# Four graph layers on one core: layer 2's product with the squared adjacency as three reduced-precision passes over split operands

## The chip, the cores and the metric

The kernel runs on one core of a Trainium2 chip. TensorE (PE) does the matrix products and writes to PSUM, which has eight banks of 512 fp32 columns per partition; VectorE (DVE), ScalarE (ACT) and GpSimd (POOL) do the rest; SyncE (SP) issues nearly all transfers. The metric is the device time of one launch in microseconds (us), lower is better. Each engine works through its own list of instructions in order and waits on semaphores for the others.

## The reference

The input x has 32 matrices of 512 nodes by 128 features; adj is one 512 x 512 matrix, about an eighth of it nonzero. Four layers follow one another, each of the form x = x + gnn(relu(layernorm(x))). All of it is fp32. Layer 0 is an attention over adj, layer 1 a Chebyshev filter over adj, layer 3 an attention with a tanh-limited score, masked by adj. The change touches layer 2. There `coeff` and `A` are both adj, so the weights are adj squared element by element:

```python
def _L2_gnn_ref(H, A, coeff, psi_w, psi_b, phi1_w, phi1_b, phi2_w, phi2_b):
    weights = coeff * A
    features = jax.nn.relu(jnp.einsum('bnd,de->bne', H, psi_w) + psi_b)
    messages = jnp.einsum('nm,bnd->bmd', weights, features)
    phi_in = jnp.concatenate((messages, H), axis=-1)
    h = jax.nn.relu(jnp.einsum('bnk,kd->bnd', phi_in, phi1_w) + phi1_b)
    return jnp.einsum('bnd,de->bne', h, phi2_w) + phi2_b
```

and the call is `x = x + _L2_gnn_ref(h, adj, adj, ...)`.

## The kernel before

**Tiles.** The 32 matrices are handled in 16 pairs q; x stays in SBUF for the whole run. A matrix is four tiles of 128 nodes by 128 features. Layers 0 and 1 combine two pairs (a block r of four matrices, eight blocks), layers 2 and 3 go pair by pair.

**Products with a 512 x 512 matrix.** Such a product is written as a 2 x 2 block product with seven multiplications instead of eight (the Winograd form of Strassen's scheme). `sum_steps` (L301) makes sums of the left matrix's quarters once, into a tile with the tag "sums"; `right_steps` (L345) makes four differences of the right operand for each pair, in tiles with the tag "rt", on POOL. `products` (L365) then runs seven steps in the order of `ORDER`, which share three PSUM banks a, c and d: a later step adds to a bank that an earlier one has filled, after an eviction has read it. `mixed` (L393) is the form for one pair: each step is two FP32 matmuls of 256 columns (L379), and the evictions (ACT copies L400 and L408, DVE additions L402 to L419) put the result together.

**Layer 2 for a pair** (`layer2`, a generator that stops at each `yield`): normalise (ACT, L247); turn the result to feature-major with DVE transposes and two trips through DRAM on SP's queue (L283 to L292); multiply with psi, add the bias on DVE and apply relu on ACT (L1063, L1064); four POOL differences (L356); the seven-step product with sq (L379), which yields msgT; phi_2's bias onto x on POOL (L1075); phi_1 (L1080, L1081), whose relu writes over msgT (L1082); phi_2 (L435) and the addition to x (L1086); statistics for the next layer (L227).

**The square.** `square` (L1139) is a generator too. Its first step loads adj into the tile sq (tag "square", four buffers of 8 KB per partition), in an order of rows that suits the transposition by 32 x 32 blocks, and loads the transposed adj, needed by layer 3 as a mask, into adjTx. Four further steps multiply one quarter of sq with itself on POOL and copy it back; then come the four sums. All this happens while layer 1 still runs.

**Order.** Layer 0 keeps its source order. From there on a list-scheduling framework sets the order of each engine's instructions from the order in which the program emits them and from what it holds to be ready; buffers of a tag are handed out as they come free. The program emits in rounds: each round advances every active generator by one step, the older ones first, and starts one more. `square` starts in the sixth round, one round after layer 1's block 3:

```python
    waiting = [[next_layer, layer1(1), layer0_stats()]]
    for r in range(2, NQ // 2):
        waiting += [[], [layer1(r)]]
    waiting[5].append(square())
```

In a steady round of layer 2, PE has pair q's product, then psi for pair q+1, phi_2 for pair q-1 and phi_1 for pair q.

**Buffers that the change touches.** "rt": six tiles of 2 KB per partition, used for the differences in layers 0, 1 and 2 and for a temporary of layer 1. "quad": two tiles of about 8 KB, used by layer 0's g, layer 1's w (the weighed features of a block, copied from PSUM by ACT at L958), layer 2's msgT and layer 3's operands. "square": four tiles of 8 KB, used among others by adj_s, x1T (layer 1's product), sq, adjTx and layer 3's exponentials. "hs": six tiles of 2 KB.

Of the kernel before, what the change touches and what calls it, by code (L numbers as in the profile page):

```python
# [8 lines left out]

F32 = mybir.dt.float32  # L10
F16 = mybir.dt.float16
BF16 = mybir.dt.bfloat16
AF = mybir.ActivationFunctionType
OP = mybir.AluOpType
AX = mybir.AxisListType

P = 128
QR = 32
NQR = P // QR
NEG = 9000000000000000.0  # L20
EPS = 1e-5


@with_exitstack
def kernel(
# [37 lines left out]
    nc = tc.nc  # L63
    B, N, D = x.shape
    NT = N // P
# [4 lines left out]
    const = ctx.enter_context(tc.tile_pool(name="const", bufs=1))  # L70
# [3 lines left out]
    work = ctx.enter_context(tc.tile_pool(name="work", bufs=4))  # L74
    bounce = ctx.enter_context(tc.tile_pool(name="bounce", bufs=4, space=bass.MemoryType.DRAM))

    def bank(name):
        return psum.tile([P, 512], F32, tag="bank", name=name)

# [7 lines left out]
    def square_tile(name):  # L87
        return const.tile([P, NT, N], F32, tag="square", name=name, bufs=4)

    def crossed(ap):  # L90

        return ap.rearrange("p (a b c) -> p b a c", a=NT, b=NQR)

    def split(ap):
        return ap.rearrange("p (a b c) -> p a b c", a=NT, b=NQR)

    def load_crossed(dst, src):
        for b in range(NQR):
            tc.keep_in_program_order(
                nc.sync.dma_start(dst[:, b, :], src.rearrange("(a b c) w -> b a c w", a=NT, c=QR)[b]))  # L100
# [91 lines left out]
    shift, scale = {}, {}  # L192
# [105 lines left out]
    H = N // 2  # L298
    sums = {}

    def sum_steps(mat, name, eng=nc.gpsimd):  # L301

        a11, a12 = mat[:, 0:2, 0:H], mat[:, 2:4, 0:H]
        a21, a22 = mat[:, 0:2, H:N], mat[:, 2:4, H:N]
        extra = const.tile([P, 3, 2, H], F32, tag="sums", name=f"sums_{name}", bufs=2)
        s1, s2, s4 = extra[:, 0], extra[:, 1], extra[:, 2]
        sums[name] = {1: a11, 2: a12, 3: s4, 4: a22, 5: s1, 6: s2, 7: a21}
        for out, op, p, q in ((s1, OP.add, a21, a22), (s2, OP.subtract, s1, a11),
                              (a21, OP.subtract, a11, a21), (s4, OP.subtract, a12, s2)):
            tc.keep_in_program_order(eng.tensor_tensor(out, p, q, op))  # L310
            yield
# [6 lines left out]
    def att_sums():  # L318

        a11, a12 = attT[:, 0:2, 0:H], attT[:, 2:4, 0:H]  # L320
        a21, a22 = attT[:, 0:2, H:N], attT[:, 2:4, H:N]
        extra = const.tile([P, 3, 2, H], F32, tag="sums", name="sums_att", bufs=2)
        s1, s2, s4 = extra[:, 0], extra[:, 1], extra[:, 2]
        sums["att"] = {1: a11, 2: a12, 3: s4, 4: a22, 5: s1, 6: s2, 7: a21}
        yield
        for out, p, bank_of, half, first in ((s1, a21, 2, 1, False), (s2, s1, 0, 0, False),
                                             (a21, a21, 0, 0, True), (s4, s2, 2, 0, True)):
            for k in range(2):
                b = pt[bank_of + k][:, half * H : half * H + H]
                if out is s1:  # L330
                    nc.vector.tensor_add(out[:, k], b, p[:, k])
                elif first:
                    nc.vector.tensor_sub(out[:, k], b, p[:, k])
                else:
                    nc.vector.tensor_sub(out[:, k], p[:, k], b)
            yield

    def right_blocks(half, name, engs):

        right = {}  # L340
        for _ in right_steps(half, name, engs, right):
            pass
        return right
# [21 lines left out]
    def products(name, form, left, right, evict, order=ORDER, on=lambda k, p: p):  # L365


        banks = {}
        for k, g, first in order:
            if first:  # L370
                banks[g] = bank(f"p_{name}_{g}")
            form(on(k, banks[g]), left[k], right[k], first)
            evict(k, banks[g])
            yield
# [18 lines left out]
    def mixed(name, left, right, dst):  # L393

        m1 = dst[:, 0, H:], dst[:, 1, :H], dst[:, 1, H:]

        def evict(k, p):
            p = p[:, :H]
            if k == 1:
                nc.scalar.copy(m1[0], p)  # L400
            elif k == 6:
                nc.vector.tensor_add(m1[1], p, m1[0])  # L402
            elif k == 7:
                nc.vector.tensor_add(m1[2], p, m1[0])
            elif k == 5:
                return
            elif k == 2:
                nc.scalar.copy(dst[:, 0, :H], p)  # L408
            elif k == 4:
                nc.vector.tensor_add(dst[:, 0, H:], p, m1[0])  # L410
            elif k == 3:
                nc.vector.tensor_add(dst[:, 1, :H], p, m1[1])

        def evict2(k, p):
            evict(k, p)
            if k == 5:
                held.append(p)
            if k == 7:
                nc.vector.tensor_add(dst[:, 1, H:], held[0][:, :H], m1[2])  # L419

        held = []
        return products(name, by_feature, left, right, evict2)

    def at(hT, b):
        return lambda t: hT[:, t, b, :]
# [13 lines left out]
    def quad_tile(name):  # L439
        return work.tile([P, 2, 2 * N + 2 * NT], F32, tag="quad", name=name, bufs=2)  # L440
# [36 lines left out]
    adjT_d = bounce.tile([N, N], F32, tag="adjT", name="adjT_d", bufs=1)  # L477
# [38 lines left out]
    for t in range(NT):  # L516
        for s in range(t + 1):
            nc.tensor.matmul(pi[:, t : t + 1], upto[:, s, blk(t)], rch[:, s : s + 1],
                             start=(s == 0), stop=(s == t))

    p = bank("p_qk_t")
# [28 lines left out]
    for i in range(3):  # L550
        eh = prep.tile([P, NK], BF16, name=f"eh_{i}")
        nc.gpsimd.tensor_copy(eh, ecoln)
        part = prep.tile([P, NK], F32, name=f"part_{i}")
# [11 lines left out]
    for t in range(NT):  # L565
        s = prep.tile([P, NE], F16, tag="lt", name=f"lt_{t}", bufs=2)
# [3 lines left out]
        for j in range(NT):  # L570
            nc.tensor.matmul(pg[j // 2][:, j % 2, :], m[:, t, blk(j)], of_row[:, t, :],
                             start=(t == 0 and j % 2 == 0), stop=(t == NT - 1), skip_group_check=True)
    pb = bank("p_known")[:, : 2 * NK].rearrange("p (k e) -> p k e", e=2)
    for kk in range(NK):
        for t in range(NT):
            nc.tensor.matmul(pb[:, kk, :], of_row[:, t, blk(kk)], known[:, t, :],
                             start=(t == 0), stop=(t == NT - 1))
# [17 lines left out]
    for kk in range(NK):  # L595
        for j in range(NT):
            nc.tensor.matmul(pw[kk][:, j * P :], pgs[:, j, blk(kk)], upto[:, j, j * P :],
                             start=(j == 0), stop=(j == NT - 1), skip_group_check=True)
# [10 lines left out]
    for kk in range(NK):  # L609
        s = prep.tile([P, N], F16, tag="scr", name=f"scr_c{kk}", bufs=2)  # L610
# [427 lines left out]
    def layer1_stats():  # L1038

        ln_stats(NQ - 2)  # L1040
        yield
        ln_stats(NQ - 1)
# [10 lines left out]
    def layer2(q):  # L1053
        h = normed(q)
        yield
        hT = transposed(h, f"hT2_{q}")
        yield
        yield
        feat = []
        for b in range(2):  # L1060
            pf = projected(f"p_feat_{q}_{b}", (at(hT, b), psi))
            feat.append(late.tile([P, NT, D], F32, tag="hs", name=f"feat_{q}_{b}", bufs=6))
            nc.vector.tensor_add(feat[b], pf, spread(psib, NT))  # L1063
            nc.scalar.activation(feat[b], feat[b], AF.Relu)  # L1064
        right = right_blocks(lambda J, b: feat[b][:, 2 * J : 2 * J + 2, :], f"feat_{q}", [nc.gpsimd] * 4)
        yield
        if q % 2 == 0:
            msgs.append(quad_tile(f"msgT_{q}"))
        msgT = msgs[-1][:, q % 2, : 2 * N].rearrange("p (b w) -> p b w", b=2)
        for _ in mixed(f"msgT_{q}", sums["sq"], right, msgT):  # L1070
            pass
        for b in range(2):
            for i in range(0, NT, 2):
                xi = xt[q][:, b, i : i + 2, :]
                tc.keep_in_program_order(nc.gpsimd.tensor_add(xi, xi, spread(phi2b, 2)))  # L1075
        yield
        h1T = msgT
        for b in range(2):
            ph = bank(f"p_phi1_{q}_{b}")
            nc.tensor.matmul(ph, phi1[:, 1, :], hT[:, :, b, :], start=True, stop=False)  # L1080
            nc.tensor.matmul(ph, phi1[:, 0, :], msgT[:, b], start=False, stop=True)  # L1081
            nc.scalar.activation(crossed(h1T[:, b]), split(ph), AF.Relu, bias=phi1b)  # L1082
        yield
        for b in range(2):
            po = projected(f"p_l2_{q}_{b}", (columns(h1T[:, b]), phi2))
            nc.vector.tensor_add(xt[q][:, b], po, xt[q][:, b])  # L1086
        ln_stats(q)
# [46 lines left out]
            if not final:  # L1134
                nc.sync.dma_start(out_r, xt[q][:, b])

    adjTx = []

    def square():  # L1139

        sq = square_tile("sq")
        load_crossed(sq, adj)
        adjTx.append(square_tile("adjTx"))
        load_crossed(adjTx[0], adjT_d)
        yield
        for i in range(NT):
            s = late.tile([P, N], F32, tag="hs", name=f"sq_{i}", bufs=6)
            nc.gpsimd.tensor_mul(split(s), crossed(sq[:, i, :]), crossed(sq[:, i, :]))
            nc.gpsimd.tensor_copy(sq[:, i, :], s)
        yield from sum_steps(sq, "sq")  # L1150

    next_layer = layer1(0)
    for r in range(NQ // 2):
# [8 lines left out]
    waiting[-1].append(layer2(0))  # L1162
    waiting += [[layer2(q)] for q in range(1, NQ)]
    waiting[-NQ + 7].append(layer1_stats())
    waiting += [[layer3(q)] for q in range(NQ)]
    active = []
    while waiting or active:
# [37 lines left out]
```

## Time and profile before

| what | value |
|---|---|
| time, median of 3 runs | 963.69 us (963.59 to 963.74) |
| span of the profiled execution | 961.7 us |
| granted TensorE clock, mean | 1.000 |
| HBM read / written | 44.17 / 40.89 MB |

The span is from the first to the last instruction; the runs' time is 2.0 us longer. Busy time by stage (a stage's borders are blurred, since the layers overlap):

| stage | us | PE busy | DVE | ACT | POOL |
|---|---|---|---|---|---|
| layer 0, 0 to 180 | 180 | 175.9 | 144.8 | 97.5 | 143.6 |
| layer 1, 180 to 445 | 265 | 264.1 | 150.4 | 96.4 | 107.2 |
| layer 2, 445 to 670 | 225 | 224.8 | 144.0 | 124.5 | 92.7 |
| layer 3, 670 to 962 | 292 | 288.6 | 145.2 | 150.7 | 80.3 |

All waits of PE on another engine that the profile shows sum to 4.9 us, the longest 2.0 us at the start. An FP32 matmul appears as two weight loads (PEld) and two matmul records, and the recorded durations overlap, because matmuls are pipelined: the distance between starts is the time that one takes.

### The profile page before, as it was taken

How to read it: one execution, taken by the hardware profiler on the slowest of the kernel's cores; microseconds unless marked ns; L12 is line 12 of the kernel's file. 1: busy time of each engine (PE TensorE's matmuls, PEld its weight loads, DVE VectorE, ACT ScalarE, POOL GpSimd, SP SyncE). 2: the span in 40 equal slices, each digit the busy share in tenths (PEclk: the TensorE clock that was granted, in tenths of full speed). 3: DMA queues.
4: the chain of work that ended last, by engine and by line, in shares of the span. 5: the costliest groups of instructions: out<-in, count | busy, mean ns of one | idle time of the engine just before them, and what ended most of it. 6: DMA issues, size and time to landing. Idle time of an engine off the chain costs nothing.

```text
span 961.7 us, 15152 instructions
## 1 busy us (share of the span) xinstructions
PE 953.3 (99%) x5465; PEld 780.8 (81%) x5465; DVE 584.4 (61%) x1326; ACT 469.1 (49%) x1054; POOL 423.8 (44%) x470
## 2 busy tenths in 40 slices
PE   8999999999999999999999999999999999999998
PEld 4899999898989999899877777777677777767776
DVE  8888885846536545656667665665654444444444
ACT  5865542442232233277627655444765445544553
POOL 5878987833517522513333444433032233223322
PEclk9999999999999999999999999999999999999999
DMA  9356532441341230343333433223121121211111
GB/s 252 62 166 185 160 108 84 104 110 55 102 136 45 66 88 23 110 110 96 89 99 97 126 91 85 74 82 88 56 88 56 55 77 44 72 61 45 55 33 44
DMA packets 83913, 86.04 MB, mean 89 GB/s; under 512 B 6784, under 2 KB 74624, under 8 KB 83840
## 3 DMA queue, kind: packets, MB, share of 16 engines
q1 hardware_dynamic: 83552, 84.57, 31.6%
q8 instruction: 43, 0.70, 0.3%
q10 hardware_dynamic: 288, 0.52, 0.2%
q14 instruction: 30, 0.25, 0.1%
HBM read 44.17 MB, written 40.89 MB: 88 GB/s over the span
## 4 chain that ended last, share of the span: by engine, by line
PE 96%; ACT 2%; DVE 1%; DMA 0%; POOL 0%; issue 0%; DVEq 0%; ACTq 0%
PE p_av L1125 12%; PE p_score L1110 11%; PE p_l_c L386 8%; PE p_w L435 6%; PE p_l_d L386 6%; PE p_msgT_c L379 5%; PE p_l_a L386 4%; PE p_x1T_c L379 4%; PE p_l L435 3%; PE p_feat L435 3%; PE p_hv L435 3%; PE p_qkh L1097 3%; PE p_x1T_a L379 3%; PE p_msgT_d L379 3%; PE p_g L435 3%; PE p_x1T_d L379 3%
## 5 line engine op out<-in xcount | busy, mean ns | idle before, releaser
L247 ACT ACTIVATE h<-x,sh,rs 128x128 f32<-128x128 f32 x512 | 209.2, 484 | 51.7 <-PE p_x1T_d L379 21.7
L1115 POOL TENSOR_TENSOR ex<-ex,adjTx 128x512 f32<-128x512 f32 x62 | 80.3, 1295 | 208.3 <-ACT ex L1113 202.8
L1111 ACT ACTIVATE ex<-p_score 128x512 f32<-128x512 f32 x128 | 71.9, 587 | 122.8 <-issue 113.0
L1125 PEld LDWEIGHTS p_av<-qkh_hv,ex 128*128 128x128 f32 x1024 | 118.4, 191 | 8.4 <-issue 7.4
L1125 PE MATMUL p_av<-qkh_hv,ex 128*128 128x129 f32 x1024 | 119.9, 274 | 0.0
L1110 PE MATMUL p_score<-qkh_hv,hT 128*128 128x512 f32 x256 | 115.2, 593 | 0.0
L283 DVE STREAM_TRANSPOSE hb_hT<-h 128x512 f32<-128x512 f32 x120 | 82.0, 698 | 23.7 <-ACT h L247 22.6
L1115 DVE TENSOR_TENSOR ex<-ex,adjTx 128x512 f32<-128x512 f32 x66 | 46.1, 703 | 82.0 <-ACT ex L1113 81.9
L227 DVE BATCH_NORM_STATS2 bn<-x 128x6 f32<-128x256 f32 x248 | 89.8, 419 | 0.6
L1110 PEld LDWEIGHTS p_score<-qkh_hv,hT 128*128 128x128 f32 x256 | 46.2, 190 | 46.5 <-issue 44.5
L1113 ACT ACTIVATE ex<-ex 128x512 f32<-128x512 f32 x128 | 76.7, 630 | 1.9
L356 POOL TENSOR_TENSOR rt_feat<-feat,feat 128x256 f32<-128x256 f32 x16 | 11.6, 725 | 136.4 <-ACT feat L1064 136.4
L958 ACT COPY w<-p_w 128x512 f32<-128x512 f32 x32 | 18.2, 574 | 106.1 <-PE p_w L435 106.1
L356 POOL TENSOR_TENSOR rt_w<-w,rt_w 128x512 f32<-128x512 f32 x16 | 20.4, 1273 | 110.3 <-DVE rt_w L356 92.0
L435 PE MATMUL p_w<-th,x1T 128*128 128x128 f32 x256 | 49.5, 275 | 0.0
L435 PE MATMUL p_w<-th,hs 128*128 128x128 f32 x256 | 49.5, 275 | 0.0
L435 PEld LDWEIGHTS p_hv<-vw,hT 128*128 128x128 f32 x256 | 33.6, 192 | 15.3 <-issue 8.1
L1075 POOL TENSOR_TENSOR x<-x,phi2b 128x256 f32<-128x256 f32 x64 | 44.5, 727 | 0.0
L435 PEld LDWEIGHTS p_w<-th,hs 128*128 128x128 f32 x256 | 39.9, 192 | 0.7
L1064 ACT ACTIVATE feat<-feat 128x512 f32<-128x512 f32 x32 | 20.1, 629 | 41.4 <-DVE feat L1063 41.4
L1130 DVE SCALAR_TENSOR_TENSOR x<-p_av,rsum,x 128x128 f32<-128x128 f32 x128 | 39.1, 347 | 1.9
L712 POOL TENSOR_TENSOR hd<-hT,adiag 128x512 f32<-128x512 f32 x32 | 39.6, 1274 | 0.2 <-ACT adiag L838 0.2
(238 smaller groups left out, 2039.7 us busy)
## 6 DMA issues: line engine op xcount, KB each, us to landing
d_hT<-hb_hT SPq DMA_DIRECT2D x240, 128.0 KB
hT<-d_hT SPq DMA_DIRECT2D x60, 512.0 KB
x<-in_x_dram SPq DMA_DIRECT2D x32, 256.0 KB
out_dram<-x SPq DMA_DIRECT2D x31, 256.0 KB
adjT_d<-adj_squares SPq DMA_DIRECT2D x4, 256.0 KB
sq<-in_adj_dram SPq DMA_DIRECT2D x4, 256.0 KB
adjTx<-adjT_d SPq DMA_DIRECT2D x4, 256.0 KB
adj_s<-in_adj_dram ACTq DMA_DIRECT2D x2, 256.0 KB
```

The costliest lines, as they stand in the source:

```text
L227: nc.vector.bn_stats(st[:, k].rearrange("p e s -> p (e s)"), xt[q][:, b, t : t + 2, :].rearrange("p t f -> p f t"))
L247: nc.scalar.activation(h[:, b, t, :], xt[q][:, b, t, :], AF.Relu, bias=shift[q][:, i : i + 1], scale=scale[q][:, i : i + 1])
L283: nc.vector.transpose(hb[:, :, b].rearrange("p j t r -> p t j r"), h[:, b].rearrange("p t (j c) -> p t j c", c=QR))
L379: nc.tensor.matmul(p[:, :H], b[:, k, :], a[:, k, :], start=(first and k == 0), stop=(k == 1), skip_group_check=True)
L386: nc.tensor.matmul(p[:, i * 2 * D : (i + 1) * 2 * D], a[:, k, blk(i)], b[:, k], start=(first and i == 0 and k == 0), stop=(k == 1), skip_g ...
L435: nc.tensor.matmul(p[:, blk(t)], hT(t), w, start=(i == 0), stop=(i == len(terms) - 1))
L1075: tc.keep_in_program_order(nc.gpsimd.tensor_add(xi, xi, spread(phi2b, 2)))
L1110: nc.tensor.matmul(ps, hT[:, t, b, :], qkh, start=True, stop=True)
L1111: nc.scalar.activation(ex[:, t, :], ps, AF.Tanh, scale=1.0 / (8.0 * math.sqrt(D)))
L1113: nc.scalar.activation(ex[:, t, :], ex[:, t, :], AF.Exp, scale=8.0)
L1115: eng.tensor_mul(split(ex[:, t, :]), split(ex[:, t, :]), crossed(adjTx[0][:, t, :]))
L1125: nc.tensor.matmul(po[:, i, : D + 1], ex[:, t, blk(i0 + i)], hv[:, t, :], start=(t == 0), stop=(t == NT - 1))
```

## The change

The numbers for layer 2's product are split. A value x is written as high + low, where both fit the reduced fp32 format (`float32r`) of TensorE, and the product of two such sums is put together from three products of parts: high with high, low with low, and mid with mid, where mid is a combination of the two parts (scale factors make the cross terms come out). Each part product is a matmul with `float32r` operands, 512 columns wide, and all twelve of one matrix add into one PSUM bank. The scheme of seven block products isn't used here any more.

```diff
+F32R = mybir.dt.float32r
+PARTS = ("high", "low", "mid")
+LOW = 4096.0
+DOWN = 1.0 - 1.0 / 8192.0
+UP = 1.0 + 1.0 / 4096.0
...
-        extra = const.tile([P, 3, 2, H], F32, tag="sums", name=f"sums_{name}", bufs=2)
+        extra = const.tile([P, 4, 2, H], F32, tag="sums", name=f"sums_{name}", bufs=2)
...
+    def moving_parts(x, high, low, mid):
+
+        nc.scalar.activation(high, x, AF.Copy, scale=DOWN)
+        nc.gpsimd.tensor_sub(low, x, high.bitcast(F32))
+        nc.vector.scalar_tensor_tensor(mid, x, 1.0 / UP, high.bitcast(F32), OP.mult, OP.subtract)
...
+    def fixed_parts(x, high, low, mid):
+
+        nc.scalar.activation(high, x, AF.Copy, scale=DOWN)
+        nc.gpsimd.tensor_sub(x, x, high.bitcast(F32))
+        nc.scalar.activation(low, x, AF.Copy, scale=LOW)
+        nc.gpsimd.tensor_sub(mid, high.bitcast(F32), low.bitcast(F32))
+
+    def mixed_parts(name, left, right, dst):
+
+        p = bank(f"p_{name}")
+        for part in range(3):
+            for t in range(NT):
+                nc.tensor.matmul(p, right[part][:, t, :], left[part][:, t, :],
+                                 start=(t == 0 and part == 0), stop=(t == NT - 1 and part == 2))
+        nc.scalar.activation(dst, p, AF.Copy, scale=UP)
```

In `layer2` the differences become parts, and the product is called once for each matrix of the pair:

```diff
-        right = right_blocks(lambda J, b: feat[b][:, 2 * J : 2 * J + 2, :], f"feat_{q}", [nc.gpsimd] * 4)
+        right = [[work.tile([P, NT, D], F32R, tag="rt", name=f"feat_{part}_{q}_{b}", bufs=6) for part in PARTS]
+                 for b in range(2)]
+        for b in range(2):
+            moving_parts(feat[b], *right[b])
         yield
...
-        for _ in mixed(f"msgT_{q}", sums["sq"], right, msgT):
-            pass
+        for b in range(2):
+            mixed_parts(f"msgT_{q}_{b}", sq, right[b], msgT[:, b])
```

`square` loads adj into a "quad" tile instead of a "square" one, and writes the three parts of the square: high and low into "square" tiles, mid into the second "sums" tile, which becomes as large as a square (8 KB instead of 6). The mask's load moves into a generator of its own that starts with the last but one pair of layer 2:

```diff
+        raw = quad_tile("adj_crossed").rearrange("p w e -> p (w e)")[:, : 4 * N]
+        raw = raw.rearrange("p (t n) -> p t n", t=NT)
+        load_crossed(raw, adj)
+        sq.extend(const.tile([P, NT, N], F32R, tag="square", name=f"sq_{part}", bufs=4) for part in PARTS[:2])
+        sq.append(const.tile([P, NT, N], F32R, tag="sums", name=f"sq_{PARTS[2]}", bufs=2))
+        yield
+        for i in range(NT):
+            s = late.tile([P, N], F32, tag="hs", name=f"sq_{i}", bufs=6)
+            nc.gpsimd.tensor_mul(split(s), crossed(raw[:, i, :]), crossed(raw[:, i, :]))
+            fixed_parts(s, *(part[:, i, :] for part in sq))
+            yield
+
+    def load_mask():
+
+        yield
         adjTx.append(square_tile("adjTx"))
         load_crossed(adjTx[0], adjT_d)
-        yield
-        for i in range(NT):
-            s = late.tile([P, N], F32, tag="hs", name=f"sq_{i}", bufs=6)
-            nc.gpsimd.tensor_mul(split(s), crossed(sq[:, i, :]), crossed(sq[:, i, :]))
-            nc.gpsimd.tensor_copy(sq[:, i, :], s)
-        yield from sum_steps(sq, "sq")
...
+    waiting[-2].append(load_mask())
```

A further function, `scaled_parts`, is added and not called. In the order that the scheduler gives the changed program, PE's list is the one of before with the product blocks exchanged (and psi of pairs 1 and 7, a part of which stood inside a product block, moved behind it). On ACT, around block 3 of layer 1, the list reads: high of quarter 0, low of quarter 0, high of quarters 1 and 2, first copy of w, two square roots, low of quarters 1 and 2, second copy of w, first copy of x1T of pair 7. On POOL it reads: multiplication of quarter 0, copy of hs, last difference of layer 1's pair 9, subtraction and mid of quarter 0, copy of hs, multiplications of quarters 1 and 2, their subtractions, their mids with two copies of hs between and after. Quarter 3 follows one block later.

More of the change, by code (lines that the diff above doesn't have):

```diff
@@ L321, in att_sums @@
         a21, a22 = attT[:, 0:2, H:N], attT[:, 2:4, H:N]
-        extra = const.tile([P, 3, 2, H], F32, tag="sums", name="sums_att", bufs=2)
+        extra = const.tile([P, 4, 2, H], F32, tag="sums", name="sums_att", bufs=2)
         s1, s2, s4 = extra[:, 0], extra[:, 1], extra[:, 2]
@@ L422, in mixed, with scaled_parts @@
         return products(name, by_feature, left, right, evict2)
+    def moving_parts(x, high, low, mid):
+        nc.scalar.activation(high, x, AF.Copy, scale=DOWN)
+        nc.gpsimd.tensor_sub(low, x, high.bitcast(F32))
+        nc.vector.scalar_tensor_tensor(mid, x, 1.0 / UP, high.bitcast(F32), OP.mult, OP.subtract)
+    def scaled_parts(x_low, high, low, mid):
+        nc.scalar.activation(high, x_low, AF.Copy, scale=DOWN / LOW)
+        nc.vector.scalar_tensor_tensor(low, high.bitcast(F32), -LOW, x_low, OP.mult, OP.add)
+        nc.gpsimd.tensor_sub(mid, high.bitcast(F32), low.bitcast(F32))
[3 more added lines that the diff above has]
+        nc.scalar.activation(low, x, AF.Copy, scale=LOW)
+        nc.gpsimd.tensor_sub(mid, high.bitcast(F32), low.bitcast(F32))
+    def mixed_parts(name, left, right, dst):
[5 more added lines that the diff above has]
+        nc.scalar.activation(dst, p, AF.Copy, scale=UP)
     def at(hT, b):
@@ L1135, in layer3 @@
                 nc.sync.dma_start(out_r, xt[q][:, b])
-    adjTx = []
+    adjTx, sq = [], []
     def square():
[L1141 to L1144, printed above, removed]
+        raw = quad_tile("adj_crossed").rearrange("p w e -> p (w e)")[:, : 4 * N]
[3 more added lines that the diff above has]
+        sq.append(const.tile([P, NT, N], F32R, tag="sums", name=f"sq_{PARTS[2]}", bufs=2))
         yield
@@ L1147, in square @@
             s = late.tile([P, N], F32, tag="hs", name=f"sq_{i}", bufs=6)
-            nc.gpsimd.tensor_mul(split(s), crossed(sq[:, i, :]), crossed(sq[:, i, :]))
-            nc.gpsimd.tensor_copy(sq[:, i, :], s)
-        yield from sum_steps(sq, "sq")
+            nc.gpsimd.tensor_mul(split(s), crossed(raw[:, i, :]), crossed(raw[:, i, :]))
[3 more added lines that the diff above has]
+        yield
+        adjTx.append(square_tile("adjTx"))
+        load_crossed(adjTx[0], adjT_d)
     next_layer = layer1(0)
```

## Prediction

> **What bounds the kernel now.** I read the page first (busy shares, then the chain that ended last), then the PE timeline of a steady layer 2 round, then the ACT, POOL and PE timelines of the stretch in which the square of adj is made, since the change adds work there.
>
> ```profile
> PE 953.3 (99%) x5465; PEld 780.8 (81%) x5465; DVE 584.4 (61%) x1326; ACT 469.1 (49%) x1054; POOL 423.8 (44%) x470
> PE 96%; ACT 2%; DVE 1%; DMA 0%; POOL 0%; issue 0%; DVEq 0%; ACTq 0%
> ```
>
> TensorE is busy for 99% of the span and is 96% of the chain; nothing else comes near. So the time falls by what leaves PE, and rises by any idle time the change puts into PE. The PE timeline of one round of layer 2:
>
> ```profile
> 610.69 1.03 PE L379 MATMUL p_msgT_a<-sq,feat 128*128 128x256 f32 x4
> 611.56 1.03 PE L379 MATMUL p_msgT_c<-sums_sq,rt_feat 128*128 128x256 f32 x4
> 612.42 1.03 PE L379 MATMUL p_msgT_d<-sums_sq,rt_feat 128*128 128x256 f32 x4
> 613.41 1.13 PE L379 MATMUL p_msgT_c<-sq,rt_feat 128*128 128x256 f32 x4
> 614.38 1.03 PE L379 MATMUL p_msgT_a<-sq,feat 128*128 128x256 f32 x4
> 615.24 1.03 PE L379 MATMUL p_msgT_c<-sq,rt_feat 128*128 128x256 f32 x4
> 616.11 1.03 PE L379 MATMUL p_msgT_d<-sums_sq,feat 128*128 128x256 f32 x4
> 616.97 1.95 PE L435 MATMUL p_feat<-psi,hT 128*128 128x128 f32 x16
> 618.75 1.95 PE L435 MATMUL p_l<-phi,msgT 128*128 128x128 f32 x16
> 620.54 1.02 PE L1080 MATMUL p_phi<-hT,phi 128*128 128x512 f32 x2
> ...
> 623.98 1.03 PE L379 MATMUL p_msgT_a<-sq,feat 128*128 128x256 f32 x4
> ```
>
> Starts are what counts (the durations include the pipeline). The seven products take 616.97 - 610.69 = 6.28 us: 28 records at 0.216 (0.865 for four) are 6.05, and the rest is PE waiting for a DVE eviction. The other operations of the round take 7.0 us. The second place, where layer 1 works beside the making of the square:
>
> ```profile
> 294.40 2.48 POOL L1148 TENSOR_TENSOR sq<-sq 128x512 f32<-128x512 f32 x2
> 297.23 0.59 ACT L958 COPY w<-p_w 128x512 f32<-128x512 f32 x1 [16.42 <-PE p_w L435]
> 298.96 0.59 ACT L958 COPY w<-p_w 128x512 f32<-128x512 f32 x1 [0.39 <-PE p_w L435]
> 299.83 0.37 ACT L400 COPY x1T<-p_x1T_a 128x256 f32<-128x256 f32 x1 [0.28 <-PE p_x1T_a L379]
> 301.35 1.03 PE L379 MATMUL p_x1T_c<-adj_s,rt_h 128*128 128x256 f32 x4
> ```
>
> ACT has idled 16 us and copies each result the moment PE has it. The PE line at 301.35 is the second use of bank c; it needs the DVE addition that follows the ACT copy of 299.83. Here ACT is in front of PE.
>
> **What the Trainium skill says.** "FP8 and Floating Point Precision", section "TensorE Precision Notes": true FP32 makes four passes through the array, while a reduced form reads 4-byte values and truncates them. The trace agrees on the first: an FP32 product of 512 columns takes 0.859 us (L1080, two records), four times the 0.215 us of a bf16 product of 512 columns (six of L635 in 1.29 us). The reduced form is in no run yet. "PSUM — Partial Sum Buffer", section "Engine vs sequencer instructions": ACT, DVE and POOL queues are strict FIFO; the trace shows each engine in program order. "TensorE: Matmul & The Clock Gate", section "HAM oscillation — how this bites in real kernels": PE gaps over about 3.4 us bring the clock down to half. No run here shows it: PE's longest wait is 2.0 us and its clock 1.000.
>
> **The change, part by part.**
>
> *Layer 2's product on PE.* Out: the sixteen blocks of L379 on msgT, 6.05 to 6.56 us each by their starts in the timeline, 99.9 us in all, DVE waits included. In: per pair 24 products of 512 columns in single passes (2 matrices, 3 parts, 4 row tiles). The operation isn't in the trace. By the nearest rows (bf16 0.215, FP32 0.215 a pass, 0.216 a record with its load) I take 0.216: 5.18 us a pair, 82.9 in all. Gain 17.0 us. The bound below is 0.213, 1 us more gain; nothing suggests that columns go in faster. Above, the weight load might stop hiding: as recorded it takes 0.190 us, 0.406 together. But PE's 128-column FP32 records start 0.112 us apart with such a load each, so 0.213 us of streaming covers it.
>
> *Parts of feat.* Out per pair: four POOL subtractions of 256 (0.73 each) and evictions (two ACT copies of 0.36, five DVE additions of 0.42). In: per matrix one ACT scaling, one POOL subtraction and one DVE operation of 512, then one ACT copy from PSUM: by like rows 0.63 (L1064), 1.27 (L310), 0.69 (L996) and 0.58 (L958). Per pair ACT +1.7, POOL -0.4, DVE -0.7 us, against rounds of about 12.2 us; ACT is busy for 23.5 of the 50 us from 600 to 650 now, 6.2 a round. On the path they cost nothing: with t=0 at the end of a product block, PE ends feat at 0.9 and 1.8; DVE adds to 2.6, ACT (relu, high, relu, high) ends at 4.3, POOL's two low parts at 5.6, DVE's two mid parts (behind the l2 additions, which wait for PE until 3.6) at 5.6. The next product starts at 7.0, with high; low comes 0.9 later. A cover of 1.4 us. The six part tiles fill all six rt buffers, so high parts wait for the products of the pair before; these have ended by t=0. At the join with the last block of layer 1, which wants four rt tiles, DVE's mid of pair 1 waits for a product of that block, and the addition queued behind it for a free bank: ready 13.7 us after the start of pair 0's product, PE asks at 13.9. Nothing, or a few tenths.
>
> *Making the square.* POOL still has twelve operations (multiplication, two subtractions each, instead of multiplication, copy and the sums). New are eight ACT scalings of 0.63 that wait for POOL, and in ACT's new order six stand around the two copies of p_w and ahead of the x1T copy of 299.83. Walked on the clock of before:
> - POOL: sq_0 294.40 to 295.65, an hs copy (0.61) and a subtraction of layer 1 (0.69) that stand between, first subtraction to 298.2 (ACT's high is long done).
> - ACT: low_0 to 298.9. POOL: mid_0 to 300.2, hs to 300.8, sq_1 to 301.9, sq_2 to 302.9 (1.04 each).
> - ACT: high_1, high_2 to 303.6, first p_w copy to 304.1, two sqrt (0.3 each) to 304.7, low_1 to 305.3. POOL: two subtractions, 304.2 and 305.4.
> - ACT: low_2 to 306.1, second p_w copy 306.7, x1T copy 307.0. DVE adds to 307.5; PE goes on at 307.55 instead of 301.35.
>
> So PE stands still for 6.2 us. Behind the waiting ACT instructions are layer 1's copies and the next normalisation; all engines move by the same amount, and a PE that is full to the end never gives it back. The fourth quarter (35 us later) delays the x1T copy by 0.8 us against a slack of some 0.6: 0.2 us. Bounds: 4 us if POOL's operations run nearer 1.0 than 1.27; 8 if DVE holds POOL up (its first multiplication took 1.49).
>
> *The clock after that gap.* An estimate from the clock-gate page: half speed for about 3.4 us of renewed work, a loss of 1.7 us. Bounds 0 (no throttle) and 3.4 (windows badly placed). As the gap is nearly twice 3.4 us, I take 1.7.
>
> *Loads.* SP now loads adj after hT of pair 7 and no longer adjTx there: 11.5 us less of queue in front of the pair 7 stores, needed by nobody early. The load waits for a quad buffer (the w of block 1, done about 259) and POOL wants it at 294. Buffer w of block 4 then waits for the last multiplication, included above. The four adjTx issues move into layer 2's late rounds, ahead of pair 15's hT load; both have at least three rounds, over 30 us, until use. Nothing.
>
> *Sum:* -17.0 + 6.2 + 0.2 + 1.7 = -8.9 us. The profiled span is 961.7, so 952.8; the median shown is 963.69, 2.0 us over the span for what lies around it: 954.8 us.
>
> **Rivals.**
> - *The square's chain does not stop PE* (12%): if POOL is quick or ACT's copies get through, the whole gain stays: 963.7 - 17.0 = 946.7, 946 to 950. For it: only three ACT-POOL handovers need be faster. Against: ACT's order puts a POOL multiplication ahead of the first copy in any case.
> - *The new matmuls are not single passes at full rate* (11%): slower. One mechanism, at L458: if 512 columns take 0.43 us (two passes, or a load that isn't hidden), 384 of them take 165 us, +65, with the gap +73: about 1037. It decides from (99.9 - 8.1)/384 = 0.239 us an instruction. For it: the operand type is in no row. Against: same bytes per column as one FP32 pass, which takes 0.215. This also covers a change that doesn't do what it says.
> - *Layer 2 gets waits of its own* (7%): the six rt buffers leave no spare, and a cover of 1.4 us is thin; 0.4 us lost in each of 16 pairs gives about 961, still just faster.
>
> **How the numbers follow.** The forecast, 954.8, has 70%: 951 to 958 by the bounds above. Range 946 to 960: the forecast's case and the first rival, with part of the third; outside stays the slow one and little else. Faster by over 0.2% 0.87, within 0.2% 0.02 (0.2%, 1.9 us, is about what a measurement of this kernel can tell from no change), slower 0.11.
>
> **What would show it.** Right: L458 records about 0.216 us apart and one each; product blocks of 5.2 us, rounds of 12.2; a wait of PE on DVE near 301 of some 6 us with ACT's scalings in front of it, and a clock below 1.0 just behind. Wrong: records above 0.239 us apart, waits of p_msgT on POOL, DVE or ACT in each round, or no gap at 301.

## The result and the profile after

| | runs | median us | lowest to highest | ratio to before, 95% interval |
|---|---|---|---|---|
| before (first series) | 4 | 963.64 | 963.53 to 963.74 | |
| after (first series) | 4 | 961.38 | 961.04 to 962.54 | 0.9979 [0.9965, 0.9993] |
| before (beside e1 to e4 below) | 17 | 963.67 | 963.48 to 964.43 | |
| before (beside e5 to e7) | 25 | 963.59 | 963.37 to 964.50 | |
| after (the same, run e6 below) | 21 | 961.99 | 961.20 to 963.56 | 0.9982 [0.9976, 0.9989] |

The change makes the kernel faster by about 0.2%: 1.6 us by the longer series, 2.3 by the short one. The forecast was 8.9 us. The profiled execution has a span of 960.8 us, 0.9 less than before. The experiments are set against the longer series of the changed kernel (961.99), also those that ran beside the 17; the kernel before differs by 0.08 us between the two.

The page of the changed kernel, first the busy times, then the granted clock in 40 slices, then the chain that ended last:

```profile
PE 946.0 (98%) x5401; PEld 772.9 (80%) x5401; DVE 588.8 (61%) x1278; ACT 497.8 (52%) x1094; POOL 437.0 (45%) x438
...
PEclk9999999999998999999999999999999999999999
...
PE 93%; POOL 3%; ACT 2%; DVE 1%; issue 1%; DMA 0%; POOLq 0%; ACTq 0%; DVEq 0%
```

PE still sets the end. One slice of the clock, the thirteenth (288 to 312 us), is no longer full. The chain runs through POOL for 3% now, but this share doesn't measure a loss: experiment e1 takes the stall shown next away, and its page has POOL at 4%. The PE timeline of the slice (start, length, instruction, and in brackets the idle time before it and who ended it):

```profile
300.43 1.03 PE L384 MATMUL p_x1T_d<-sums_adj,rt_h 128*128 128x256 f32 x4
307.67 2.07 PE L384 MATMUL p_x1T_c<-adj_s,rt_h 128*128 128x256 f32 x4 [6.21 <-DVE x1T L407]
309.54 1.91 PE L384 MATMUL p_x1T_a<-adj_s,h 128*128 128x256 f32 x4
311.24 1.91 PE L384 MATMUL p_x1T_c<-adj_s,rt_h 128*128 128x256 f32 x4
312.95 1.38 PE L384 MATMUL p_x1T_d<-sums_adj,h 128*128 128x256 f32 x4
314.17 1.03 PE L384 MATMUL p_x1T_a<-adj_s,h 128*128 128x256 f32 x4
```

The same blocks before (the one at 301.35 stands in the prediction):

```profile
300.49 1.03 PE L379 MATMUL p_x1T_d<-sums_adj,rt_h 128*128 128x256 f32 x4
304.81 1.03 PE L379 MATMUL p_x1T_a<-adj_s,h 128*128 128x256 f32 x4
```

PE stands still for 6.21 us, and the four blocks behind that take 314.17 - 307.67 = 6.50 us by their starts; before, they took 304.81 - 301.35 = 3.46. So 3.0 us more are lost after the stall. The ACT timeline of the same stretch shows what the DVE addition had been waiting for:

```profile
298.79 0.63 ACT L450 ACTIVATE sq_low<-sq 128x512 fp32r<-128x512 f32 x1 [2.29 <-POOL sq L449]
302.34 0.63 ACT L448 ACTIVATE sq_high<-sq 128x512 fp32r<-128x512 f32 x1 [2.93 <-POOL sq L1190]
303.34 0.63 ACT L448 ACTIVATE sq_high<-sq 128x512 fp32r<-128x512 f32 x1 [0.37 <-POOL sq L1190]
303.88 0.57 ACT L996 COPY w<-p_w 128x512 f32<-128x512 f32 x1
...
304.74 0.62 ACT L450 ACTIVATE sq_low<-sq 128x512 fp32r<-128x512 f32 x1
305.78 0.63 ACT L450 ACTIVATE sq_low<-sq 128x512 fp32r<-128x512 f32 x1 [0.42 <-POOL sq L449]
306.32 0.57 ACT L996 COPY w<-p_w 128x512 f32<-128x512 f32 x1
306.78 0.38 ACT L405 COPY x1T<-p_x1T_a 128x256 f32<-128x256 f32 x1
```

Five scalings of the square stand there ahead of the x1T copy; the brackets show ACT idle for POOL in front of four of them. The copy starts at 306.78 and not at 299.83 as before.

Now a round of layer 2, PE timeline (the last line has three of its four records, because the window asked for ends there):

```profile
600.04 1.02 PE L1122 MATMUL p_phi<-msgT,phi 128*128 128x512 f32 x2
600.50 1.49 PE L458 MATMUL p_msgT<-sq_high,feat_high 128*128 128x512 f32 x4
601.82 1.10 PE L458 MATMUL p_msgT<-sq_low,feat_low 128*128 128x512 f32 x4
602.75 1.10 PE L458 MATMUL p_msgT<-sq_mid,feat_mid 128*128 128x512 f32 x4
...
605.55 1.09 PE L458 MATMUL p_msgT<-sq_mid,feat_mid 128*128 128x512 f32 x4
606.49 1.95 PE L473 MATMUL p_feat<-psi,hT 128*128 128x128 f32 x16
...
613.09 1.26 PE L458 MATMUL p_msgT<-sq_high,feat_high 128*128 128x512 f32 x3
```

The view prints f32 for these products; their operands are the `float32r` tiles, which other lines print as fp32r. Each product is one record and takes about half of the 0.43 us of an FP32 record, which holds two of the four passes; so it is a single pass. But four of them take 0.93 us: (606.49 - 601.82) / 20 = 0.2335 us each, and not 0.216. The first group's 1.32 us is not a longer product: its first record begins while the last product of phi is still streaming. Counted from phi's start, 600.04 + 0.86 (phi) + 4 x 0.2335 = 601.83, and the next group starts at 601.82. The whole round shows it as well. From 600.50 to 613.09 it takes 12.59 us, where the round shown of before takes 13.29 (623.98 - 610.69); less the 7.0 us of the other operations that leaves 5.59, which is 24 times 0.233. Sixteen pairs at 24 x 0.2335 = 5.60 make 89.7 us in place of 99.9: the product gives 10.2 us, not 17.0.

Two of the three groups of weight loads of L458 (busy time, mean ns of one, then the idle time before them and what ended most of it):

```profile
L458 PEld LDWEIGHTS p_msgT<-sq_high,feat_high 128*128 128x128 f32 x128 | 24.1, 189 | 11.4 <-issue 6.9 <-ACT msgT L1123 0.2
...
L458 PEld LDWEIGHTS p_msgT<-sq_low,feat_low 128*128 128x128 f32 x128 | 23.9, 188 | 6.0 <-POOL feat_low L437 0.4
```

Waits for parts of feat are 0.4 us in the whole kernel, so the missing time isn't there.

Each product is dearer by 17.5 ns, in every round alike: from the start of one group of four to the next, the first group of each pair's block aside, it is 0.92 to 0.94 us in 79 of 80 cases (the other took 1.00). Nor does it hang on the other engines: over the 352 distances between neighbouring products of layer 2 the first of each block aside, the mean is 0.233 us, and it is 0.233 beside a busy POOL and beside an idle one, and the same for ACT and DVE. The granted clock is 1.00 in all of layer 2.

The account closes. PE starts layer 2's first product 9.45 us later than before (460.90 against 451.45 us); nearly all of it is the stall with its slow blocks (314.17 - 300.43 = 13.74 us, where before took 304.81 - 300.49 = 4.32). From there to the end of its last product layer 2 takes 208.55 us instead of 218.94, 10.4 less. Together that is 0.9 less, as between the two spans. Two things were left to show: that stall and slow blocks have the causes given, and what the 17.5 ns belong to.

### The profile page after: what moved, and what is told of

It reads as the page before. It is cut to its first block, busy times and chain, and to the rows that moved or that the text cites. A ratio compares the mean times of both kernels' runs of the same rounds, so it can differ in the third digit from the quotient of the medians.

```text
span 960.8 us, 14971 instructions
## 1 busy us (share of the span) xinstructions
PE 946.0 (98%) x5401; PEld 772.9 (80%) x5401; DVE 588.8 (61%) x1278; ACT 497.8 (52%) x1094; POOL 437.0 (45%) x438
## 4 chain that ended last, share of the span: by engine, by line
PE 93%; POOL 3%; ACT 2%; DVE 1%; issue 1%; DMA 0%; POOLq 0%; ACTq 0%; DVEq 0%
PE p_av L1166 12%; PE p_score L1151 11%; PE p_msgT L458 9%; PE p_l_c L391 8%; PE p_l_d L391 5%; PE p_w L473 5%; PE p_x1T_c L384 4%; PE p_l_a L391 4%; PE p_l L473 3%; PE p_feat L473 3%; PE p_hv L473 3%; PE p_phi L1121 3%; PE p_qkh L1138 3%; PE p_phi L1122 3%; PE p_g L473 3%; PE p_x1T_a L384 3%
## 5 line engine op out<-in xcount | busy, mean ns | idle before, releaser
L437 POOL TENSOR_TENSOR feat_low<-feat,feat_high 128x512 fp32r<-128x512 f32 x32 | 50.5, 1595 | 118.1 <-ACT feat_high L436 108.7
L238 ACT ACTIVATE sd<-bn,eps 128x8 f32<-128x8 f32 x62 | 18.7, 304 | 60.6 <-DVE bn L232 54.8
L1116 POOL TENSOR_TENSOR x<-x,phi2b 128x256 f32<-128x256 f32 x64 | 49.6, 805 | 0.0
L384 PE MATMUL p_x1T_c<-adj_s,rt_h 128*128 128x256 f32 x128 | 35.6, 403 | 6.5 <-DVE x1T L407 6.4
L458 PE MATMUL p_msgT<-sq_high,feat_high 128*128 128x512 f32 x128 | 41.1, 443 | 0.0
```

The lines of the kernel that those rows point to most:

```text
L384: nc.tensor.matmul(p[:, :H], b[:, k, :], a[:, k, :], start=(first and k == 0), stop=(k == 1), skip_group_check=True)
L458: nc.tensor.matmul(p, right[part][:, t, :], left[part][:, t, :], start=(t == 0 and part == 0), stop=(t == NT - 1 and part == 2))
```

## Experiments

**e1: one quarter of the square in each of four blocks.** Rival explanations were that the handovers cost the same anywhere, or that the wait is off the path.

```diff
             fixed_parts(s, *(part[:, i, :] for part in sq))
-            yield
+            for _ in range(3 if i == 0 else 2):
+                yield
```

> The same work as the changed kernel; only the four quarters of the square are put one in each of four blocks of layer 1, instead of three in one block and one in the next. Theory (the stall of 6.2 us and the slow blocks behind it come from three quarters standing together ahead of the x1T copy on ACT): each quarter costs what the fourth one costs now, about 0.2 us, and the clock stays at 1.0: 961.4 - 6.2 - 3.0 + 0.6 = 952.8 us. Rival (the handovers cost the same wherever they stand): four waits of 1.5 us, no slow blocks: 958.4 us. Rival (the wait is not on the path): 961.4 us.

Measured: 954.47 us (4 runs, 954.13 to 955.48), ratio to before 0.9906 [0.9892, 0.9920]. Its PE timeline where the stall was:

```profile
300.51 1.03 PE L384 MATMUL p_x1T_d<-sums_adj,rt_h 128*128 128x256 f32 x4
301.64 1.13 PE L384 MATMUL p_x1T_c<-adj_s,rt_h 128*128 128x256 f32 x4
302.60 1.03 PE L384 MATMUL p_x1T_a<-adj_s,h 128*128 128x256 f32 x4
```

The six-microsecond hole is gone, the blocks behind take 0.86 us, and the list of waits names one for x1T only, 0.3 us at 187 us, which stands there before the change too (0.2). The same instructions on the same engines are 7.5 us faster than the changed kernel (961.99) by where they stand. Both rivals fall. It is 1.7 us above the 952.8 expected. 0.6 of it comes because the changed kernel is rather at 962.0 than at 961.4, and 0.4 to 0.7 because its slow blocks cost 2.3 to 2.6 us in the later runs (e5, e6) and not 3.0. The rest is that a quarter costs more than 0.2 us. In the lines above, 302.60 - 300.51 = 2.09 us, where before took 1.73 (two blocks of 0.864); the other three quarters take the same to 0.01 us, and so does the fourth quarter of the changed kernel. That is about 0.36 us each, of which the trace shows only 0.08 to 0.10 as waiting.

**e2: products of 256 columns.** It separates a price per weight load from a price per column.

```diff
-                nc.tensor.matmul(p, right[part][:, t, :], left[part][:, t, :],
-                                 start=(t == 0 and part == 0), stop=(t == NT - 1 and part == 2))
+                for c in range(2):
+                    nc.tensor.matmul(p[:, c * H : c * H + H], right[part][:, t, :], left[part][:, t, c * H : c * H + H],
+                                     start=(t == 0 and part == 0 and c == 0), stop=(t == NT - 1 and part == 2),
+                                     skip_group_check=True)
```

> Each product of 512 columns of the layer 2 message is issued as two of 256, so 48 weight loads a pair and not 24, with the same columns. In the changed kernel one of 512 takes 0.233 us where 0.216 was forecast. Theory A (a fixed cost of 17.5 ns with every weight load): 24 x 16 x 0.0175 = 6.7 us more, 968 us, starts of the 256-column products 0.125 us apart. Theory B (the columns go in more slowly, 0.455 ns each): no change, 961.4 us, 0.117 us apart. Theory C (a load of 0.188 us is hidden only where the streaming is longer): 48 x 0.19 = 9.1 us a pair instead of 5.6, 1017 us, 0.19 us apart.

Measured: 963.56 us (12 runs), ratio 0.9996 [0.9988, 1.0005], 1.6 us above the changed kernel. PE timeline:

```profile
602.38 1.11 PE L459 MATMUL p_msgT<-sq_low,feat_low 128*128 128x256 f32 x8
603.33 1.10 PE L459 MATMUL p_msgT<-sq_mid,feat_mid 128*128 128x256 f32 x8
...
607.10 1.95 PE L475 MATMUL p_feat<-psi,hT 128*128 128x128 f32 x16
```

(607.10 - 602.38) / 40 = 0.118 us for 256 columns. With 0.2335 for 512 the slope is 0.1155 us / 256 = 0.451 ns a column and the fixed part 2.5 ns a product (with the means of all distances in the two traces, 0.2329 and 0.1180, it is 0.449 and 3 ns). Theory A asked for 0.125 and 968 us, C for 0.19 and 1017; both fall. B holds but for the small fixed part, which 24 x 16 additional products pay once more (about 1.0 us, most of the 1.6). It also shows that a load recorded at 188 ns doesn't hold up products 118 ns apart.

**e3: the parts in float16.** Same products, order and banks; only the operands are half as wide (the bitcasts of the parts to F32 go as well).

```diff
-    right = [[work.tile([P, NT, D], F32R, tag="rt", name=f"feat_{part}_{q}_{b}", bufs=6) for part in PARTS]
+    right = [[work.tile([P, NT, D], F16, tag="rt", name=f"feat_{part}_{q}_{b}", bufs=6) for part in PARTS]
...
-    sq.extend(const.tile([P, NT, N], F32R, tag="square", name=f"sq_{part}", bufs=4) for part in PARTS[:2])
-    sq.append(const.tile([P, NT, N], F32R, tag="sums", name=f"sq_{PARTS[2]}", bufs=2))
+    sq.extend(const.tile([P, NT, N], F16, tag="square", name=f"sq_{part}", bufs=4) for part in PARTS[:2])
+    sq.append(const.tile([P, NT, N], F16, tag="sums", name=f"sq_{PARTS[2]}", bufs=2))
```

> The three parts of feat and of the square are float16 instead of fp32r; instructions and their order on the other engines stay. The parts are rounded differently by this. Theory A (the 17.5 ns above 0.216 belong to the 4-byte operands or to their weight load): 0.216 us a product, 5.2 us a block, 961.4 - 6.7 = 954.7 us, a little less if ACT, POOL and DVE also write the narrow parts faster. Theory B (they belong to 24 products in a row into one bank, or to other engines' traffic): 0.233 us and 961.4 us.

Measured: 955.25 us (4 runs, 955.00 to 955.51), ratio 0.9912 [0.9899, 0.9926]. PE timeline:

```profile
596.12 1.03 PE L458 MATMUL p_msgT<-sq_high,feat_high 128*128 128x512 f16 x4
596.98 1.03 PE L458 MATMUL p_msgT<-sq_low,feat_low 128*128 128x512 f16 x4
...
601.30 1.95 PE L473 MATMUL p_feat<-psi,hT 128*128 128x128 f32 x16
...
608.31 1.03 PE L458 MATMUL p_msgT<-sq_high,feat_high 128*128 128x512 f16 x4
```

A group takes 0.864 us, a product (601.30 - 596.98) / 20 = 0.216, a block 5.18 and a round 12.19: the forecast's figures to the hundredth, with another operand type. 16 x 24 x 0.0175 = 6.7 us, and the medians differ by 961.99 - 955.25 = 6.7. So the 17.5 ns come with the `float32r` operands, and not with 24 products into one bank or with the engines beside them alone (theory B); with e2, they are nearly all a price per column. That it is the width of 4 bytes as such is not shown: the type changes with it. Layer 1's stall is still in this kernel; it is 0.4 us shorter (5.8 us), and two blocks of layer 2 that take 5.24 and 5.50 us instead of 5.18 cost about as much.

**e4: a filled gap, first attempt.** Seven unused products were meant to keep PE busy through the wait. They were tied to the name of matrix pair 8's x1T; the wait is in pair 7's.

```diff
+            if k == 7 and name == "x1T_8":
+                idle = bank("p_idle")
+                for _ in range(7):
+                    nc.tensor.matmul(idle, adj_s[:, 0, blk(0)], adj_s[:, 0, :], start=True, stop=True)
```

> Seven fp32 products of adj_s, 0.86 us each, stand on PE ahead of the product that waits near 301; their result goes into a bank that nobody reads. They add work that isn't used. Theory (the four slow blocks after the stall are the clock, which comes down because PE is idle for 6.2 us): the blocks after the wait take 0.86 us each again, 3.0 us less: 958.4 us. Rival (these blocks are slow for another reason, such as traffic of ACT and POOL): 961.4 us.

Measured: 967.94 us (5 runs), ratio 1.0044 [1.0031, 1.0057]. Its PE timeline:

```profile
307.58 2.08 PE L388 MATMUL p_x1T_c<-adj_s,rt_h 128*128 128x256 f32 x4 [6.22 <-DVE x1T L411]
...
316.24 2.31 PE L380 MATMUL p_idle<-adj_s 128*128 128x512 f32 x5
```

The filler stands 8.7 us behind the start of the product that waited, where nothing had to be filled (five of its 14 records lie in the window asked for). So it says nothing on the clock; it shows that on a full PE 6.0 us of added work (7 x 0.859) cost 6.0 us (967.94 - 961.99).

**e5: the gap filled.** The same with "x1T_7".

> The seven unused fp32 products of the run before (0.86 us each, 6.0 us) now stand one product of layer 1 earlier, where the wait is: between the third and the fourth block of x1T at 300 to 308. They add work that isn't used. Theory (the slow blocks behind the stall are the clock, because PE was idle): PE is busy through the wait, the wait left is 0.2 us, the blocks behind it take 0.86 us each and not 1.9, 1.7 and 1.7: 2.6 to 3.0 us less than the changed kernel in the trace. Rival (the slow blocks come from what ACT and POOL do then): the wait goes, the slow blocks stay, and the time is that of the changed kernel.

Measured: 959.68 us (5 runs, 959.60 to 959.75), ratio 0.9958 [0.9946, 0.9971]. PE timeline:

```profile
300.57 1.03 PE L388 MATMUL p_x1T_d<-sums_adj,rt_h 128*128 128x256 f32 x4
301.43 6.17 PE L380 MATMUL p_idle<-adj_s 128*128 128x512 f32 x14
307.81 1.13 PE L388 MATMUL p_x1T_c<-adj_s,rt_h 128*128 128x256 f32 x4 [0.21 <-DVE x1T L411]
308.78 1.03 PE L388 MATMUL p_x1T_a<-adj_s,h 128*128 128x256 f32 x4
```

The product that waited comes at 307.81, 0.14 us later than in the changed kernel, ACT and POOL do what they did, and the blocks behind it run at full speed. The kernel does 6 us more work and is 2.3 us faster than the changed one (961.99). The granted clock agrees. Here are two stretches of 10 us in the changed kernel and then in e5 (borders, length, busy time of PE, PEld, DVE, ACT and POOL, granted clock, DMA):

```profile
300.00:310.00 10.00, 3.79 (x13) 2.84 (x12) 2.96 (x6) 4.03 (x9) 9.30 (x10) 0.84 0.00 0
310.00:320.00 10.00, 10.00 (x41) 8.49 (x40) 3.97 (x9) 4.20 (x11) 0.00 (x0) 0.82 0.06 13
...
300.00:310.00 10.00, 9.79 (x32) 5.67 (x31) 3.61 (x7) 4.18 (x10) 9.45 (x10) 1.00 0.00 0
310.00:320.00 10.00, 10.00 (x59) 8.99 (x58) 4.34 (x10) 5.88 (x16) 0.00 (x0) 1.00 0.22 54
```

The slow blocks are the clock of a PE that was idle, and not what ACT and POOL do then.

**e6: the changed kernel again,** as the zero of this series.

> The changed kernel itself once more, beside the two others on the same chip, so that the differences of a few us have their own zero. Every theory: 961.4 us, or up to 1 us more, since its first four runs spread from 961.0 to 962.5.

Measured: 961.99 us, in the table above. Its profile has the stall at 6.21 us and slow blocks of 1.87, 1.71 and 1.65 us by their starts, a loss of 2.6 us, where the first profile had 3.0.

The clock records of the traces show why the loss differs (narrow stretches of the view just used give the borders). All five traces with the stall have one stretch at half clock:

| trace | clock at 0.5, us | PE back at | work at half clock | lost by the starts |
|---|---|---|---|---|
| after, first profile | 306.83 to 313.66 | 307.67 | 5.99 | 3.0 |
| e2 | 306.12 to 312.95 | 307.68 | 5.27 | 2.7 |
| e3 | 305.35 to 312.17 | 307.21 | 4.96 | 2.5 |
| e4 | 305.86 to 312.69 | 307.58 | 5.11 | 2.6 |
| e6 | 305.95 to 312.78 | 307.61 | 5.17 | 2.6 |

The stretch is 6.83 us long each time; what differs is where it lies, and the loss is about half of the part that falls on work. In all nine traces the time from one change of the clock to the next is a whole multiple of 3.41 us (6.83 is two, the 300.37 us of full clock ahead of it are 88, the 955.73 of before are 280). So the clock changes on a grid of steps of 3.41 us, whose place differs from one execution to the next. In the first profile the steps end at 303.42, 306.83, 310.24 and 313.66 us, and PE has no work from 301.46 to 307.67. The clock fell at the end of the first whole step without work and came back at the end of the first whole step of work, and so it did in the other four traces.

**e7: both edits, e1 and e3.**

> The two edits that each took time off, together: one quarter of the square in each of four blocks of layer 1, and the parts in float16 (they are rounded differently by this). If the stall with its slow blocks and the price of a product are the two causes and don't touch each other, the gains add up: 954.5 - 6.1 = 948.3 us, rounds of layer 2 of 12.2 us. Rival (at 12.2 us a round the thin cover of 1.4 us no longer holds and PE waits for POOL's or ACT's parts): 0.3 us or more in each of 16 rounds, 953 us.

Measured: 947.51 us (5 runs, 947.46 to 947.81), ratio 0.9832 [0.9819, 0.9846], 16.1 us faster than the kernel before and 14.5 faster than the changed one. Page and PE timeline:

```profile
PE 937.1 (99%) x5401; PEld 735.6 (78%) x5401; DVE 584.8 (62%) x1278; ACT 496.5 (52%) x1094; POOL 430.4 (45%) x438
```

```profile
600.71 1.03 PE L458 MATMUL p_msgT<-sq_high,feat_high 128*128 128x512 f16 x4
...
605.88 1.95 PE L473 MATMUL p_feat<-psi,hT 128*128 128x128 f32 x16
...
612.89 1.03 PE L458 MATMUL p_msgT<-sq_high,feat_high 128*128 128x512 f16 x4
```

The round is 12.18 us and PE is 99% busy again. The gains add up (7.5 + 6.7 = 14.2 of the 14.5 us). The rival of 953 us falls: the list of waits names nothing of layer 2. The cover is not whole, though. As in e3, one of the 16 blocks takes 5.50 us and one 5.24 instead of 5.18, and in the longer of the two a product with the low part waits.

## Why the prediction was wrong

The direction was right, the size and the range were not: 961.4 lies above 960. By its own steps:

- *Layer 2's product, -17.0 us:* the step that failed. Its term "I take 0.216" was mis-sized: 0.2335, which makes -10.2. I took the price of a bf16 product and of an FP32 pass for an operand type that no row showed, and gave it a bound of 1 us below and almost none above. The argument for that, that loads hide behind 0.213 us of streaming, was right (e2); but the streaming itself is 8% slower: 0.451 ns a column, where the FP32 rows of before, worked out as in e2 (0.4295 us a record of 512 columns, 0.216 of 256, two passes each), give 0.417. A doubt of 8% in a term of 83 us is 6.7 us, and it belonged into the range. The rival "not at full rate" knew only the jump to 0.43; its own threshold of 0.239 was missed by 5 ns, and by 2 if the losses that came (9.4 us with the slow blocks) are put in place of its 8.1. So the sign came out right by a small margin, on much less than 0.87 said.
- *The stall, +6.2 us:* right by the mechanism given, with PE back at 307.67 (forecast 307.55); e1 takes it away. That it is right to 0.1 us is luck in part. POOL's first subtraction ended at 298.75 and not at 298.2, because it took 1.72 us; the links behind it, which the walk had laid end to end, overlapped a little and won 0.4 us back. The fourth quarter cost 0.35 us by the starts of the blocks (344.85 to 346.93, against 1.73), not 0.2.
- *The clock, +1.7 us:* right in kind (e5), mis-sized: 3.0 in the first profile, 2.6 in the second, 2.3 in the medians of e5 and e6. The estimate took 3.4 us of work at half clock. In five traces it was 5.0 to 6.0 (e6), so the loss of 2.5 to 3.0 lay between the 1.7 and the upper bound of 3.4. The Trainium skill's section "HAM oscillation — how this bites in real kernels" in "TensorE: Matmul & The Clock Gate" warns of half speed after such gaps, and the traces agree on the half (1.7 us for blocks of 0.86, a granted clock of 0.5). For the 3.4 us, which the estimate took from that page, the measurement decides.
  The prediction says that no run shows such a clock; the trace of before does, at its start, though its mean clock reads 1.000: the first twelve products of `p_idle` (L500), unused ones that `keep_busy` puts there, start 0.427 us apart, where the last three of the same line start 0.216 apart, and the clock record turns to 1.0 at 7.05 us, 5.05 us after the first of them (3.0 to 5.1 in the nine traces). Half of 5.05 is 2.5 us, nearer than 1.7.
- *Parts of feat, loads:* nothing, right to a few tenths: 0.4 us of waiting for parts in the changed kernel, and about 0.4 in the blocks of e7. The prices were too low: POOL's low part took 1.60 us on average and not 1.27, DVE's mid part 1.14 and not 0.69. What was left of the cover differs by pair: in most, the first low part is ready 1 to 3 us ahead of its load, but in three of the 16 the load follows POOL's write by 0.05 us.
- *Rivals:* "layer 2 gets waits of its own" named 961 us and would have been right by number alone; its mechanism costs a few tenths in all in the traces, not 0.4 us a pair. "The chain doesn't stop PE" is wrong for the changed kernel; e1 shows that it can be arranged.

With the terms put right the sum is -10.2 + 6.2 + 0.35 + 2.3 to 3.0 = -1.35 to -0.65 us; the medians say -1.6 and -2.3, the two spans -0.9. In reverse, e7 has the forecast's product and no stall: 963.6 - 17.0 = 946.6, and it measures 947.5.

Open is why a single pass over `float32r` operands streams more slowly than each of the passes of an FP32 product over operands of the same width, and whether the stationary or the moving side sets it. Neither was tried alone. The distances also scatter (0.229 to 0.241 us in the round shown, the first one aside), where those of float16 are 0.215 or 0.216; what sets that is open too.

## What to carry to other kernels

When a change moves PE to an operand type that isn't in the trace, put the uncertainty on the price per column, multiply it by the number of products, and carry it into the range; here 8% of one term was most of the gain that was forecast. Helper work that goes to and fro between two in-order engines costs what stands behind it on the queue: one quarter at a time cost about 0.36 us, three in a row cost PE 6.2 us and then 2.3 to 3.0 us of clock. An idle PE is worth a look for what follows the gap, and unused products in it can pay: here they won 2.3 us in layer 1, where nothing useful was ready, and cost their full 6.0 us where PE had no gap (e4).

## What the runs showed of the hardware

- fp32r (`float32r`), single pass, 128 x 128 weights: about 0.45 ns a column and 2.5 to 3 ns a product (0.2335 us for 512 columns, 0.118 for 256); float16 in the same place 0.216 us for 512; a pass of FP32 in the kernel before 0.417 ns a column.
- An fp32r weight load is recorded at 188 ns, a float16 one at 98 ns, yet fp32r products of 256 columns with a load each start 118 ns apart.
- After 5.8 to 6.2 us without work, the granted clock was 0.5 for 6.83 us in each of five traces. 5.0 to 6.0 us of it fell on work, and the loss of 2.5 to 3.0 us differed between executions of the same kernel (2.6 and 3.0) with the place of that stretch, on a grid of 3.41 us. With the gap filled (e5) the clock stayed at 1.0.
